# Scan layer: one more state run filled by GpSimd, state rows of 388 columns, and the output projection in a lent PSUM bank

## The chip, the cores and the metric

The kernel runs as one program on one core of a Trainium2 chip. The time is device time in microseconds (us), the median over several executions. Engines are named as in the profile: PE is TensorE (PEld its weight loads), DVE is VectorE, ACT is ScalarE, POOL is GpSimd, and SP is SyncE, which here does nothing but issue DMAs.

## The reference

The network has four layers on an input of 3 images with 256 channels of 48 x 48. Only the last, a selective scan (Mamba) layer, is touched:

```python
xz = einsum('blc,dc->bld', xn, in_proj_w); x_in, z = split(xz, 2)   # 512 channels each
u = silu(conv1d(x_in) + conv_b)                                     # 4 taps, causal
dt_raw, B_ssm, C_ssm = split(einsum('bld,ed->ble', u, x_proj_w))    # 16, 16, 16
dt = softplus(einsum('blr,dr->bld', dt_raw, dt_proj_w) + dt_proj_b)
A = -exp(A_log)                                                     # 512 x 16
def step(h, inp):                                                   # h: batch x 512 x 16
    h = h * exp(dt_t[:, :, None] * A) + dt_t[:, :, None] * B_t[:, None, :] * u_t[:, :, None]
    return h, einsum('bdn,bn->bd', h, C_t)
y = (ys + u * D_param) * silu(z)
out = einsum('bld,cd->blc', y, out_proj_w)                          # 256 channels, plus the residual x
```

The sequence of an image has 2304 tokens. Everything is fp32.

## The kernel before

The sequence is cut into chunks of 384 tokens (CH), 6 an image, 18 in all. A chunk has four channel blocks m of 128 channels, and every block two halves h of eight states each, so a chunk has **eight steps** (m, h), called the first to the eighth step here. The code counts half steps j = 0 to 15: step (m, h) holds j = 4m + 2h and the next.

In a step the 128 partitions hold 32 channels times 4 states, and the free dimension holds 8 runs of 384 tokens, indexed (g, q): two groups g of states and four quarters q of the channel block. The tile `hs` (states, L1725, three buffers) holds the runs as rows of 385 columns: the state that is carried in and 384 tokens. One step of work on a state tile is:

- **fill** (L1745): dt\*u times B is written into all eight runs before they are scanned. DVE makes the quarters q = 0, 1 (`fill_upper`, L1736). It reads dt\*u from the PSUM tile `ps_r`, two banks, one for each quarter, which `spread_pe` (L1704) writes with two matmuls of 32 rows. For h = 0 it fills both groups of its own step and the first group of the next (1536 and 768 columns), for h = 1 the second group (768). GpSimd makes q = 2, 3 of both groups in one instruction (1536 columns, L1753). It reads dt\*u from the SBUF tile `dtur`, which `spread` (L1692) loads from the DRAM tile `dtud`.
- **decay** (L1770): ACT computes exp(dt A) of one run into one of three PSUM slots, three runs ahead of the scan.
- **scan** (L1783): DVE scans one run in place (L1786). The order is q = 0, 1 of both groups, then q = 2, 3 of both.
- **times_c** (L1790): GpSimd multiplies all 3072 columns with C into `hc` (L1803).
- **add_states** (L1808): PE sums `hc` over the states into `ps_y` (L1820), after a first matmul with the diagonal of D (L1815). **gate** (L1825) multiplies with silu(z) on DVE.
- `first_states` and `last_states` carry eight columns from chunk to chunk (ACT copies, through small tiles `hst`).

The fill of the next step is issued at the end of a step, after its eight scans, and stands before `times_c` on GpSimd.

Beside the steps, the next chunks are prepared and the last one is finished. Three lists, `after`, `plan` and `gating` (L1380 to L1430), say when: each entry has a half step j, a place in it (BEGIN, MID, DONE, LATE and PE_: after the first, second, third and fourth scan, and the end of a step or of its fourth scan), a distance in chunks, and a function. `run` (L1438) calls what is due. These functions share two PSUM banks, `bank[0]` and `bank[1]`. The ones that the prediction speaks of are: project_u (PE, L1291, at j = 8, waits for ACT's silu of u), take_dbc (ACT, L1299, which also stores B and C to DRAM and loads them spread out), project_dt (PE, 17 rows, L1317, j = 8 and 10), keep_dt (ACT copies L1338, then the stores of `dtd` and `dtud`, j = 10 and 12), less_mean (PE, L1221, j = 12), centre (ACT, L1234, L1236, j = 13), square_mean (PE, L1228, j = 13), inverse_root (ACT, L1240, L1241, j = 14) and silu of z and u (ACT, with two table loads each, j = 3 and 7).

The output projection of chunk c runs while chunk c + 1 is scanned. `project_y` (L1358) adds the residual by a matmul with the identity (L1360) and four matmuls (L1362) into `bank[mo]`, one call for each half mo of the 256 output channels; `store` (L1371) copies the bank with ACT (L1372) and issues the DMA to the output:

```python
        (5, BEGIN, -1, lambda k: project_y(k, 0)),
        (6, MID, -1, lambda k: store(k, 0)),
        (7, PE_, -1, lambda k: project_y(k, 1)),
        (8, MID, -1, lambda k: store(k, 1)),
```

`keep_order` (L1889) fixes the order of PE, DVE, ACT and GpSimd to that in which the code issues its instructions; waits between engines are derived from the tiles that instructions read and write.

## Time and profile before

| what | us |
|---|---|
| median of 3 runs | 3424.14 (3421.64 to 3425.53) |
| the profiled execution | 3426.41 |
| span of the profile | 3424.6 |
| first scan begins, last scan ends | 2022.1, 3404.3 |
| busy over the span | PE 3055.3, DVE 2927.2, ACT 2378.6, POOL 1353.6 |

The profile's page gives the busy tenths of each engine in 40 slices of 85.6 us; the scan layer is the last 16 or so. Rows of groups give source line, engine, operation, names (out<-in), shapes and count, then the busy time in us, the mean of one in ns, and the idle time of the engine ahead of them with what ended it. Rows of waits give who waited for whom: us in total, how often, the longest. Rows of a timeline give start, length from the first start to the last end, engine, line, names, shape, count, and in brackets the idle time ahead. A matmul in fp32 shows as two records.

### The profile page before, as it was taken

The numbers are of one execution on the slowest core, as the hardware profiler recorded it, in microseconds if no ns is written. First come the engines' busy times: TensorE is split into PE (matmuls) and PEld (weight loads), VectorE is DVE, ScalarE is ACT, GpSimd is POOL, SyncE is SP. The second block draws the span as 40 slices with busy tenths as digits, with TensorE's granted clock in tenths as the row PEclk, the third lists the DMA queues.
The fourth block names the chain that finished last, engine by engine and source line by source line (L and its number), as shares of the span: only waits on it lengthen the run. The fifth ranks groups of instructions, "written<-read, shape, count | busy, mean of one in ns | idle before, by whom it ended". The sixth has DMA issues, their size and how long they took to land.

```text
span 3424.6 us, 51520 instructions
## 1 busy us (share of the span) xinstructions
PE 3055.3 (89%) x19882; PEld 1444.2 (42%) x19882; DVE 2927.2 (85%) x3302; ACT 2378.6 (69%) x3596; POOL 1353.6 (40%) x385
## 2 busy tenths in 40 slices
PE   7999999999999999879999978777888888877885
PEld 4334343453333435447677743333333333333331
DVE  3799899959999896479965369999999999999998
ACT  2688888848888885332224458888778888888874
POOL 0000000000000000210000039999999999999997
PEclk9999999999999999989999998888888988988887
DMA  4000000010000002756501134444454444445441
GB/s 165 28 8 10 8 8 6 12 42 5 9 9 8 7 8 82 245 165 222 192 22 37 45 104 105 110 108 122 114 121 107 116 103 113 111 109 123 121 116 43
DMA packets 167170, 272.89 MB, mean 80 GB/s; under 512 B 30129, under 2 KB 134641, under 8 KB 164994
## 3 DMA queue, kind: packets, MB, share of 16 engines
q1 hardware_dynamic: 153682, 249.44, 27.1%
q10 hardware_dynamic: 13232, 20.06, 1.8%
q8 instruction: 158, 2.59, 0.3%
q14 instruction: 98, 0.80, 0.1%
HBM read 222.08 MB, written 47.10 MB: 79 GB/s over the span
## 4 chain that ended last, share of the span: by engine, by line
PE 57%; DVE 28%; ACT 8%; issue 3%; DMA 2%; POOL 0%; SPq 0%; ACTq 0%; DVEq 0%; POOLq 0%
DVE hs L1786 17%; PE ps_s L638 16%; PE acc L651 14%; PE ps_c L1532 8%; DVE hs L1739 3%; PE ps_g L1272 3%; PE ps_g L1221 3%; PE ps_s L1031 2%; ACT ps_da L1778 2%; DVE u L296 2%; PE ps_y L462 2%; PE ps_m L665 1%; PE ps_m L711 1%; PE acc L529 1%; PE ps_s L518 1%
## 5 line engine op out<-in xcount | busy, mean ns | idle before, releaser
L642 ACT ACTIVATE pt<-ps_s 128x1024 f32<-128x1024 f32 x972 | 942.4, 1022 | 154.8 <-PE ps_s L638 142.0
L1786 DVE TENSOR_TENSOR_SCAN hs<-ps_da,hs 128x385 f32<-128x385 f32 x1152 | 1005.3, 937 | 35.2 <-ACT ps_da L1778 34.2
L857 DVE TENSOR_TENSOR part<-part,pt 128x2048 f32<-128x2048 f32 x396 | 906.6, 2289 | 41.3 <-ACT pt L642 18.5
L1778 ACT ACTIVATE ps_da<-dtr,u 128x384 f32<-128x384 f32 x1152 | 657.5, 582 | 222.9 <-DVE hs L1786 212.0
L164 POOL TENSOR_TENSOR rstd<-ve,mhalf 128x2 f32<-128x2 f32 (+1 forms) x26 | 16.3, 629 | 1479.2 <-DVE ve L162 1479.2
L638 PE MATMUL ps_s<-q,kt 32*128 32x512 f32 (+1 forms) x4320 | 576.4, 592 | 0.1
L651 PE MATMUL acc<-pt,vt 128*32 128x512 f32 (+1 forms) x4320 | 520.9, 561 | 0.2
L1803 POOL TENSOR_TENSOR hc<-hs,x 128x3072 f32<-128x3072 f32 x72 | 444.0, 6167 | 47.0 <-DVE hs L1786 38.4
L1803 POOL TENSOR_TENSOR hc<-hs,bc 128x3072 f32<-128x3072 f32 x71 | 438.0, 6169 | 42.3 <-DVE hs L1786 35.8
L1532 PE MATMUL ps_c<-vt,u 128*128 128x288 f32 x1728 | 430.4, 410 | 20.8 <-DVE u L263 20.8
L1532 PEld LDWEIGHTS ps_c<-vt,u 128*128 128x128 f32 x1728 | 329.5, 192 | 116.8 <-issue 19.7
L638 PEld LDWEIGHTS ps_s<-q,kt 32*128 32x128 f32 x4320 | 195.3, 183 | 199.1 <-issue 120.2
L1820 PE MATMUL ps_y<-hc,u 128*32 128x384 f32 x2304 | 255.4, 568 | 12.4 <-POOL hc L1803 12.4
L651 PEld LDWEIGHTS acc<-pt,vt 128*32 128x32 f32 x4320 | 94.4, 108 | 353.4 <-issue 326.7
L1272 PE MATMUL ps_g<-u 128*128 128x384 f32 x576 | 199.4, 494 | 21.3 <-ACT u L1268 21.2
L1753 POOL TENSOR_TENSOR hs<-dtur,x 128x1536 f32<-128x1536 f32 x72 | 209.1, 2905 | 7.5 <-DMA dtur<-dtud 7.5
L1753 POOL TENSOR_TENSOR hs<-dtur,bc 128x1536 f32<-128x1536 f32 x72 | 209.4, 2908 | 0.0
L1317 PE MATMUL ps_g<-wconv,u 17*128 17x384 f32 x144 | 79.2, 684 | 104.7 <-ACT x L1338 79.1
L1272 PEld LDWEIGHTS ps_g<-u 128*128 128x128 f32 x576 | 106.9, 190 | 110.8 <-ACT u L1268 42.6
L1221 PE MATMUL ps_g<-wconv,u 128*128 128x384 f32 x144 | 86.1, 770 | 63.4 <-ACT x L1338 62.9
L1820 PEld LDWEIGHTS ps_y<-hc,u 128*32 128x32 f32 x2304 | 65.5, 119 | 174.7 <-issue 153.4
L1739 DVE TENSOR_TENSOR hs<-ps_r,x 128x768 f32<-128x768 f32 (+1 forms) x108 | 127.7, 1209 | 2.9 <-DMA xd<-vt 2.8
(249 smaller groups left out, 3699.8 us busy)
## 6 DMA issues: line engine op xcount, KB each, us to landing
wconv<-in_we SPq DMA_DIRECT2D x144, 384.0 KB, 4.3
dtr<-dtd SPq DMA_DIRECT2D x288, 192.0 KB, 3.8
dtur<-dtud SPq DMA_DIRECT2D x288, 96.0 KB, 4.2
wconv<-xd SPq DMA_DIRECT2D x36, 384.0 KB, 4.8
x<-bcd SPq DMA_DIRECT2D x72, 192.0 KB, 5.3
dtd<-x SPq DMA_DIRECT2D x36, 384.0 KB, 4.8
bc<-bcd SPq DMA_DIRECT2D x72, 192.0 KB, 4.9
yc<-ycat ACTq DMA_DIRECT2D x18, 576.0 KB, 5.1
```

The lines of the kernel that those rows point to most:

```text
L638: nc.tensor.matmul(s[:, j, cols], kt[r, mt * P : (mt + 1) * P], q[r, :n], start=True, stop=True,)
L642: nc.scalar.activation(p[:, h0 : h0 + 2, :], s, AF.Exp)
L651: nc.tensor.matmul(acc[h * HD : (h + 1) * HD, :n], vt[:, mt, g * P + h * HD : g * P + (h + 1) * HD], p[:, h, cols], start=mt == 0, stop=mt ...
L857: ): nc.vector.tensor_tensor(part, first, p, ALU.add)
L1272: nc.tensor.matmul(bank[m % 2], w3v["taps"][:, m, tap, :], w3v["xi"][:, m % 3, tap : tap + CH], start=tap == 0, stop=tap == DCONV - 1,)
L1532: nc.tensor.matmul(pc[:, :HN], u[:, i, dy, ct, m * P : (m + 1) * P], vt[:, i, ct, dy * TW : dy * TW + HN], start=ct == 0 and dy == 0, stop ...
L1739: nc.vector.tensor_tensor(states(s)[:, lo:hi, 0:2, 1:], k.ps[:, :, :CH].unsqueeze(1).broadcast_to([P, hi - lo, 2, CH]), b_rows(s, lo, hi), ...
L1753: nc.gpsimd.tensor_tensor(states(s)[:, :, 2:4, 1:], chunks[at].rows[m][1].unsqueeze(1).broadcast_to([P, 2, 2, CH]), b_rows(s, 0, 2), ALU.mult,
L1778: nc.scalar.activation(slots[n % 3][:, 1 : CH + 1], chunks[at].rows[m][0][:, q, :], AF.Exp, scale=amat[:, col : col + 1],)
L1786: nc.vector.tensor_tensor_scan(b, slots[(8 * s + part) % 3][:, : CH + 1], b, 0.0, ALU.mult, ALU.add)
L1803: nc.gpsimd.tensor_tensor(hc, tiles[s][:, :, :, 1:], cb.broadcast_to([P, 2, 4, CH]), ALU.mult)
L1820: nc.tensor.matmul(k.y_ps[32 * q : 32 * q + 32, :CH], fold, hc[:, g, q, :], start=False, stop=h == 1 and g == 1,)
```

## The change

State tiles get rows of 388 columns, and the run begins at the second column. The tile from which GpSimd reads dt\*u starts every row at column 2. One of the eight runs of each second step (h = 1: g = 1, q = 1) is filled by GpSimd and no longer by DVE, whose fill shrinks from 768 to 384 columns; GpSimd reads it from a new tile `dtuq` with one buffer, which four more DMAs for each m load, and `dtud` keeps 96 instead of 64 partitions of dt\*u. The carried states move into the tile `gmat`, which was used by the earlier layers.

The output projection writes into the second bank of `ps_r` (`lent`), which DVE's fill of the second step of a block no longer reads. Its first half runs in the next chunk's fifth step in two parts (identity with m = 0, 1; then m = 2, 3), stored at the start of the sixth; its second half runs and is stored in the seventh step. The spread for m = 3 is therefore issued later, after the third scan of the sixth step.

```diff
-        d = k.dtud[m0] = dram.tile([P // 2, 2, CH], F32, name=f"dtud{m0}")
-        nc.sync.dma_start(d, k.dtu[P // 2 :, m0 : m0 + 2, :])
+        d = k.dtud[m0] = dram.tile([3 * P // 4, 2, CH], F32, name=f"dtud{m0}")
+        nc.sync.dma_start(d, k.dtu[P // 4 :, m0 : m0 + 2, :])
...
-    def project_y(k, mo, lo=0, hi=DI):
+    def project_y(k, mo, lo=0, hi=DI, into=None):
         if lo == 0:
-            nc.tensor.matmul(bank[mo], ident, k.ot[:, mo, :], start=True, stop=False)
+            k.y_out = bank[mo] if into is None else into
+            nc.tensor.matmul(k.y_out, ident, k.ot[:, mo, :], start=True, stop=False)
...
-        (5, BEGIN, -1, lambda k: project_y(k, 0)),
-        (6, MID, -1, lambda k: store(k, 0)),
-        (7, PE_, -1, lambda k: project_y(k, 1)),
-        (8, MID, -1, lambda k: store(k, 1)),
+        (8, MID, -1, lambda k: project_y(k, 0, 0, 2, lent[0])),
+        (9, BEGIN, -1, lambda k: project_y(k, 0, 2, DI)),
+        (10, BEGIN, -1, lambda k: store(k, 0, k.y_out)),
+        (12, BEGIN, -1, lambda k: project_y(k, 1, 0, DI, lent[0])),
+        (12, LATE, -1, lambda k: store(k, 1, k.y_out)),
...
-            at = 2 + m % 2
-            dtur = scn.tile([P, 2, 4 + CH], F32, name="dtur")[:, :, at : at + CH]
+            dtur = scn.tile([P, 2, 4 + CH], F32, name="dtur")[:, :, 2 : 2 + CH]
...
+        def spread_second(k, m):
+            t = scn.tile([P, 4 + CH], F32, name="dtuq", bufs=1)[:, 2 : 2 + CH]
+            for i in range(4):
+                r = slice(32 * i, 32 * i + 32)
+                nc.sync.dma_start(t[r], k.dtud[m & 2][:32, m & 1, :])
+            k.second[m] = t
...
             k.ps = t
+            lent[0] = t[:, 1, :CH]
...
-                tiles[s] = scn.tile([P, 2, 4, CH + 1], F32, name="hs", bufs=3)
+                t = scn.tile([P, 2, 4, CH + 4], F32, name="hs", bufs=3)
+                tiles[s] = t[:, :, :, 1 : CH + 2]
...
-                fill_upper(s, 1, 2)
+                fill_upper(s, 1, 2, 1)
+                nc.gpsimd.tensor_tensor(
+                    states(s)[:, 1, 1, 1:], chunks[at].second[m],
+                    chunks[at].bc[0][:, 3, :], ALU.mult,
+                )
...
-                t = state[m, h] = wp.tile([P, 8], F32, name=f"hst{m}{h}")
+                n = 8 * (2 * m + h)
+                t = state[m, h] = gmat[:, n : n + 8]
...
+                if part == 4 and h == 1 and s + 1 < len(steps):
+                    spread_second(chunks[steps[s + 1][0]], steps[s + 1][1])
...
+                if part == 2 and (m, h) == (2, 1):
+                    spread_pe(chunks[at], 3)
...
-            if h == 0 and s + 2 < len(steps):
+            if h == 0 and m != 2 and s + 2 < len(steps):
                 spread_pe(chunks[steps[s + 2][0]], steps[s + 2][1])
```

More of the change, by code (lines that the diff above doesn't have):

```diff
@@ L1200, in net, with __init__ @@
     class Chunk:
-        pass
+        def __init__(self):
+            self.second = {}
     whole = [psg.tile([P, 512], F32, name=f"ps_g{j}") for j in range(2)]
@@ L1356, in take_z @@
         nc.scalar.copy(k.sz[:, m, :], bank[j])
-    def project_y(k, mo, lo=0, hi=DI):
+    def project_y(k, mo, lo=0, hi=DI, into=None):
         if lo == 0:
-            nc.tensor.matmul(bank[mo], ident, k.ot[:, mo, :], start=True, stop=False)
+            k.y_out = bank[mo] if into is None else into
+            nc.tensor.matmul(k.y_out, ident, k.ot[:, mo, :], start=True, stop=False)
         for m in range(lo, hi):
             nc.tensor.matmul(
-                bank[mo], w("out", m * 256 + mo * P, P), k.sz[:, m, :],
+                k.y_out, w("out", m * 256 + mo * P, P), k.sz[:, m, :],
                 start=False, stop=m == DI - 1,
@@ L1369, in residual, with store @@
         nc.sync.dma_start(k.ot, xd[k.b][:, :, k.c * CH : (k.c + 1) * CH])
-    def store(k, mo):
-        nc.scalar.copy(k.ot[:, mo, :], bank[mo])
+    def store(k, mo, src):
+        nc.scalar.copy(k.ot[:, mo, :], src)
         nc.sync.dma_start(
@@ L1420, in net @@
         (2, MID, -1, residual),
-        (5, BEGIN, -1, lambda k: project_y(k, 0)),
-        (6, MID, -1, lambda k: store(k, 0)),
-        (7, PE_, -1, lambda k: project_y(k, 1)),
-        (8, MID, -1, lambda k: store(k, 1)),
+        (8, MID, -1, lambda k: project_y(k, 0, 0, 2, lent[0])),
[3 more added lines that the diff above has]
+        (12, LATE, -1, lambda k: store(k, 1, k.y_out)),
     ]
+    lent = [None]
     last_of_all = [(3, LATE, 0, lambda k: silu(k.sz))]
@@ L1694, in spread @@
             dtr = scn.tile([P, 4, CH], F32, name="dtr")
-            at = 2 + m % 2
-            dtur = scn.tile([P, 2, 4 + CH], F32, name="dtur")[:, :, at : at + CH]
-            for t, src in ((dtr, k.dtd), (dtur, k.dtud)):
-                src = src[m & 2][:, m & 1, :]
+            dtur = scn.tile([P, 2, 4 + CH], F32, name="dtur")[:, :, 2 : 2 + CH]
+            for t, src, q in ((dtr, k.dtd, 0), (dtur, k.dtud, 1)):
+                src = src[m & 2][32 * q :, m & 1, :]
                 for i in range(4):
@@ L1727, in states, with b_rows, fill_upper @@
             if s not in tiles:
-                tiles[s] = scn.tile([P, 2, 4, CH + 1], F32, name="hs", bufs=3)
+                t = scn.tile([P, 2, 4, CH + 4], F32, name="hs", bufs=3)
+                tiles[s] = t[:, :, :, 1 : CH + 2]
             return tiles[s]
-        def b_rows(s, lo, hi):
+        def b_rows(s, lo, hi, nq=2):
             at, m, h = steps[s]
             rows = chunks[at].bc[0][:, 2 * h + lo : 2 * h + hi, :]
-            return rows.unsqueeze(2).broadcast_to([P, hi - lo, 2, CH])
-        def fill_upper(s, lo, hi):
+            return rows.unsqueeze(2).broadcast_to([P, hi - lo, nq, CH])
+        def fill_upper(s, lo, hi, nq=2):
             k = chunks[steps[s][0]]
             nc.vector.tensor_tensor(
-                states(s)[:, lo:hi, 0:2, 1:],
-                k.ps[:, :, :CH].unsqueeze(1).broadcast_to([P, hi - lo, 2, CH]),
-                b_rows(s, lo, hi), ALU.mult,
+                states(s)[:, lo:hi, 0:nq, 1:],
+                k.ps[:, 0:nq, :CH].unsqueeze(1).broadcast_to([P, hi - lo, nq, CH]),
+                b_rows(s, lo, hi, nq), ALU.mult,
             )
@@ L1832, in net @@
         k.rows = {0: spread(k, 0)}
+        spread_second(k, 0)
         spread_pe(k, 0)
@@ L1882, in net @@
         for mo in range(2):
+            k.y_out = bank[mo]
             project_y(k, mo, DI - 1, DI)
-            store(k, mo)
+            store(k, mo, bank[mo])
         keep_order(tc, listed, mark)
```

## The prediction

> **What bounds the kernel now.** I read the page's slices first, then the busy times of the scan stage (first scan at 2022 us, last one ending at 3404 us), then who waits for whom in it.

> ```profile
> DVE  3799899959999896479965369999999999999998
> POOL 0000000000000000210000039999999999999997
> PEclk9999999999999999989999998888888988988887
> ...
> 2022.00:3405.00 1383.00, 1098.85 (x4583) 479.04 (x4583) 1345.46 (x1591) 1099.03 (x2134) 1292.02 (x289) 0.87 0.46 109
> ```

> The last row gives length, then busy PE, PEld, DVE, ACT, POOL, granted clock, DMA share and GB/s. DVE works 1345 of 1383 us and bounds the stage; GpSimd follows with 1292. PE is far from full, and its clock is below 1 only here.

> ```profile
> DVE hs L1786 <- ACT ps_da L1778: 34.2, 46, 0.9
> ...
> POOL hc L1803 <- DVE hs L1786: 74.2, 66, 2.9
> ```

> All that DVE waits for is ACT, some 2 us a chunk: 0.73 before the fourth scan of the third step; in the eighth step 0 to 0.9 before the fourth scan and 0.7 to 0.8 before the sixth. Consecutive chunks begin at 2720.56, 2798.15 and 2876.00, so a chunk takes about 77.7 us (every third 76.6). I work one chunk out, that of 2798.15; its eight steps begin at 2798.15, 2805.81, 2815.61, 2824.21, 2834.01, 2841.69, 2853.61 and 2863.41.

> **The run that GpSimd takes over.**

> ```profile
> L1739 DVE TENSOR_TENSOR hs<-ps_r,x 128x768 f32<-128x768 f32 x72 | 67.7, 940 | 2.8 <-DMA xd<-vt 2.8
> L1739 DVE TENSOR_TENSOR hs<-ps_r,bc 128x1536 f32<-128x1536 f32 x36 | 62.9, 1748 | 0.0
> ...
> L1803 POOL TENSOR_TENSOR hc<-hs,bc 128x3072 f32<-128x3072 f32 x71 | 438.0, 6169 | 42.3 <-DVE hs L1786 35.8 <-POOL hs L1753 6.5
> L1753 POOL TENSOR_TENSOR hs<-dtur,bc 128x1536 f32<-128x1536 f32 x72 | 209.4, 2908 | 0.0
> ```

> 768 more columns cost DVE 808 ns, so 384 fewer save 0.40 us; four times a chunk 1.6, in 18 chunks 29 us. That is the most that the change can bring. GpSimd makes a fill at 2908/1536 = 1.89 ns a column, so the new run costs 0.73 us, 2.9 a chunk: 1292 + 52 = 1344 us, still under DVE's total. The run is needed at the fourth scan of its step, while GpSimd in the fifth step ends its fill at 2841.6, five scans before the first use. I cost it at nothing; without that cover it would cost up to its own 2.9 a chunk.

> [...]

> **Rows of 388.** The product with C reads state rows of 385 columns at 2.01 ns a column; the fill reads rows of 388 at 1.89. If the stride makes the difference, the product falls to 5.81 us, 2.9 a chunk on GpSimd. No row shows these operands in the new layout, so the bounds are 5.81 and, the same difference upward, 6.53. I take the fill's rate, the nearest row with that stride. On the path it is worth 0 at 5.81 and at 6.17; at 6.53 GpSimd would need 72.1 + 2.9 + 2.9 = 77.9 a chunk and become the bound.

> **New transfers.** Four issues more for each m (0.43 us each on SP by L1701's 1.73 for four), 16 a chunk, 7 us on a queue that is mostly idle. Having one buffer, each group waits until GpSimd has read the old run, which is over more than a step earlier; store, residual and bcd issues behind it are not held. Landing takes 4.2 us (dtur's row), the use is over a step away: 0. The write of dtud grows by half, beside other work: 0. So do the state copies into gmat, same ACT copies: 0.

> **The moved output projection** is where the time goes. In the built program the TensorE order of the fifth step is: project_u; identity and m = 0, 1 of the output projection; project_dt, which waits for ACT's take_dbc; then m = 2, 3; then the sums of C. And DVE's fill at that step's end, which had no wait, now waits for the last of these matmuls: it reads bank 0 and they write bank 1 of one and the same tile. Behind that fill stand the eight scans of the sixth step, and for them ACT's decays.

> ```profile
> 2826.95 0.91 PE L1709 MATMUL ps_r<-x,u 32*128 32x384 f32 x4
> 2827.79 0.91 PE L1360 MATMUL ps_g<-wconv,ident 128*128 128x384 f32 x2
> 2828.54 2.74 PE L1362 MATMUL ps_g<-sz,u 128*128 128x384 f32 x8
> 2831.62 0.91 PE L1815 MATMUL ps_y<-x,diag 128*128 128x384 f32 x2 [0.33 <-DVE x L1827]
> 2832.46 1.50 PE L1820 MATMUL ps_y<-hc,u 128*32 128x384 f32 x16
> 2834.58 2.82 PE L1291 MATMUL ps_g<-u 128*96 128x384 f32 x8 [0.62 <-ACT u L1285]
> 2838.97 1.55 PE L1317 MATMUL ps_g<-wconv,u 17*128 17x384 f32 x4 [1.57 <-ACT wconv L1299]
> 2840.46 2.00 PE L1820 MATMUL ps_y<-hc,u 128*32 128x384 f32 x16
> ...
> 2848.40 2.92 PE L1317 MATMUL ps_g<-wconv,u 17*128 17x384 f32 x4 [4.37 <-ACT x L1338]
> 2851.25 1.65 PE L1815 MATMUL ps_y<-x,diag 128*128 128x384 f32 x2
> 2852.83 2.53 PE L1820 MATMUL ps_y<-hc,u 128*32 128x384 f32 x16
> 2859.47 5.49 PE L1221 MATMUL ps_g<-wconv,u 128*128 128x384 f32 x8 [4.11 <-ACT x L1338]
> ```

> Each fp32 matmul is two records, 0.323 us apart (L1362). *Lower end*: project_u ends at 2837.3; six records make 2839.2; project_dt 1.55, 2840.8; four records and 0.16 drain, 2842.2. DVE comes to the fill at 2840.84: **a wait of 1.35**.

> *Upper end*: the fourth step loses L1360 and L1362. TensorE, which paused 0.33 there, has nothing from the end of L1709 (2827.9 at the latest; about 2825.2, as L1709 then waits only for DVE's fill ending at 2824.2) to 2831.62: 3.8 to 6.4 us. After gaps of 4.37 and 4.11 the rows run at half speed: L1317 2.92 for 1.55, L1815 1.65 for 0.91, L1820 2.53 for 1.50, L1221 5.49 for L1291's 2.82. L1815 and L1820 would then end 1.3 later, project_u would start at 2835.9, and the wait is **2.65** (5.2 if project_u is slow as well). I take **2.2**, nearer to the slow end because the likelier gap, 6.4, is longer than both that were followed by slow rows.

> ```profile
> 2834.00:2841.70 7.70, 5.55 (x28) 2.30 (x28) 7.70 (x11) 7.30 (x15) 7.70 (x3) 0.98 0.27 70
> 2841.70:2853.60 11.90, 7.54 (x26) 2.49 (x22) 11.83 (x16) 9.72 (x20) 11.63 (x3) 0.50 0.53 114
> ```

> The granted clock falls to 0.50 right after 2841.7, with no earlier gap over 1.57 us. [...]

> The second half of the projection opens the seventh step, into L1221's gap. L1221 then runs warm and ends 2.7 earlier, which removes the fourth scan's wait in the eighth step (0, 0.6, 0.9 by chunk: 0.5). But L1228 after it may now start cold (1.56 more); I charge one in five, 0.3. The two ACT copies only change place: 0.

> **The sum, per chunk.** Fills -1.6. Of these, the first step's 0.40 returns as a longer wait in the third, since TensorE runs from 2798 to 2815 without a gap over 0.6 and feeds the ACT chain that ends there: +0.4. The seventh's returns likewise, as the ACT chain of the eighth step starts at the seventh's last scan: +0.4. New wait +2.2; eighth step -0.5 + 0.3. Total +1.2; 17 chunks make 20, and the first chunk, with no output projection behind it, gives 1 back: +19. Profiled: 3426.4 (span 3424.6 and 1.8 around it) + 19 = 3445; for the median of 3424.1, **3443 us**.

> **Rivals.**
> 1. *Faster.* TensorE stays warm in the fourth step and the two 0.4s do not return: -1.6 + 1.35 - 0.5 = -0.75 a chunk, 3410; without any wait 3395. For it: DVE is the bound and loses 29 us of work. Against: the wait is in the program. With both 0.4s returned it decides from a wait under 0.6 a chunk on, with both kept from one under 1.4. Chance 0.14.
> 2. *Nothing.* Wait at its lower end, the rest as forecast: -1.6 + 0.8 + 1.35 - 0.2 = +0.35 a chunk, 3429. Chance 0.13.
> 3. *GpSimd becomes the bound.* The product at 6.53 or the new run well over 0.73: 77.9 plus gaps a chunk; with the new wait, 3465 to 3480. Chance 0.06. If instead 388 columns do nothing (6.17), the time stays 3443, as GpSimd has room.

> **How the numbers follow.** The forecast, 3430 to 3460 (wait 1.6 to 3.2), has 0.67. Range 3416 to 3460: it leaves out the better half of rival 1, rival 3 and the wait of 5.2. Counting 0.2% (7 us), about what can be told from no change: faster 0.14, same 0.13, slower 0.73.

> **What would show it.** Right: DVE waits for PE before the 384-column fill in 17 chunks, 1.4 to 2.7 each; L1815 and L1820 slow at the fourth step's end; the third step's ACT wait up from 0.73 to about 1.1; L1221 near 2.8 us; the product with C near 5.8. Wrong: no such wait, or DVE waiting for GpSimd.

## The result and the profile after

The changed kernel takes **3440.55 us** (median of 6 runs, 3436.85 to 3442.70) against 3424.22 of the kernel before, measured beside it: ratio 1.0051, 95% interval 1.0041 to 1.0061. It is slower by 16.3 us. The forecast was 3443.

The profiled execution took 3439.55 us, 13.1 more than that of before. The scan stage itself, from the first scan to the end of the last, grew by 16.3, from 1382.2 to 1398.5. The layers ahead, which nothing touches, differ from run to run (the first scan began between 2013.9 and 2022.6 us in the profiles of this study), so the runs below are compared by their stages too. First the slices of the page, then the stage's own row (length, then busy PE, PEld, DVE, ACT, POOL, granted clock, DMA share, GB/s):

```profile
DVE  4799899859899995589965379999999999999998
...
POOL 0000000000000000110000049889999999988897
PEclk9999999999999999999999988889999988988987
```

```profile
2017.43:3415.91 1398.48, 1096.56 (x4582) 476.02 (x4582) 1317.71 (x1590) 1103.51 (x2134) 1270.15 (x361) 0.87 0.49 121
```

VectorE has 27 us less work (1345 before), and GpSimd's work fell too, by 21 (1291 before), although it has a run more to fill in half of the steps. The stage is longer all the same: VectorE now stands idle for 81 us of it, where it was 38. Its waits, then GpSimd's, in the stage:

```profile
DVE hs L1752 <- PE ps_r L1364: 43.2, 16, 2.8
DVE hs L1804 <- ACT ps_da L1796: 33.5, 36, 1.8
...
DVE hs L1804 <- POOL hs L1770: 1.4, 3, 0.8
```

```profile
POOL hs L1766 <- DMA dtuq<-dtud: 53.6, 11, 5.7
POOL hc L1821 <- DVE hs L1804: 42.6, 20, 3.1
```

The first row is new: VectorE's fill waits 16 times for the output projection. GpSimd waits for its new transfers too, but VectorE had to wait for GpSimd only three times, 1.4 us in all: GpSimd's room absorbs it. The wait in a steady chunk is seen in two timelines, of TensorE over the fourth and fifth step (2670.43 to 2690.37), and of VectorE at the end of the fifth:

```profile
2670.66 0.91 PE L1720 MATMUL ps_r<-x,u 32*128 32x384 f32 x4 [0.26 <-DVE hs L1752]
2677.83 1.65 PE L1833 MATMUL ps_y<-x,diag 128*128 128x384 f32 x2 [6.26 <-DVE x L1845]
2679.41 2.79 PE L1838 MATMUL ps_y<-hc,u 128*32 128x384 f32 x16
2682.13 2.83 PE L1292 MATMUL ps_g<-u 128*96 128x384 f32 x8
2684.79 0.81 PE L1362 MATMUL ps_r<-wconv,ident 128*128 128x384 f32 x2
2685.44 1.45 PE L1364 MATMUL ps_r<-sz,u 128*128 128x384 f32 x4
2686.82 1.55 PE L1318 MATMUL ps_g<-wconv,u 17*128 17x384 f32 x4
2688.30 1.56 PE L1364 MATMUL ps_r<-sz,u 128*128 128x384 f32 x4
```

```profile
2689.90 0.56 DVE L1752 TENSOR_TENSOR hs<-ps_r,x 128x384 f32<-128x384 f32 x1 [2.77 <-PE ps_r L1364]
```

TensorE is idle for 6.26 us of the fourth step, then L1833 and L1838 run at half speed (granted clock 0.50; 1.65 and 2.79 us, for 0.91 and 1.50 in the kernel before), and project_u (L1292), the projection and project_dt (L1318) follow without a gap up to 2689.86. VectorE's fill starts at 2689.90.

GpSimd's new run and its product with C, and VectorE's small fill:

```profile
L1821 POOL TENSOR_TENSOR hc<-hs,x 128x3072 f32<-128x3072 f32 x72 | 405.4, 5631 | 22.0 <-DVE hs L1804 22.0
...
L1766 POOL TENSOR_TENSOR hs<-dtuq,x 128x384 f32<-128x384 f32 x36 | 31.3, 869 | 43.6 <-DMA dtuq<-dtud 33.4 <-ACT ps_da L1796 5.4 <-ACT hs L1779 4.9
```

```profile
L1752 DVE TENSOR_TENSOR hs<-ps_r,x 128x384 f32<-128x384 f32 x36 | 19.4, 540 | 21.8 <-PE ps_r L1364 21.8
```

The product costs 5.63 us instead of 6.17, the run 0.87. VectorE's fill of 384 columns costs 0.54, 0.40 less than the 768.

### The profile page after: what moved, and what is told of

It is laid out like the page before. It is cut to its first block, busy times and chain, and to the rows that moved or that the text cites. A ratio compares the mean times of both kernels' runs of the same rounds, so it can differ in the third digit from the quotient of the medians.

```text
span 3437.8 us, 52144 instructions
## 1 busy us (share of the span) xinstructions
PE 3049.4 (89%) x19882; PEld 1439.2 (42%) x19882; DVE 2901.5 (84%) x3302; ACT 2383.2 (69%) x3596; POOL 1333.5 (39%) x457
## 4 chain that ended last, share of the span: by engine, by line
PE 62%; DVE 23%; ACT 6%; DMA 3%; issue 3%; POOL 1%; SPq 0%; ACTq 0%; DVEq 0%; POOLq 0%
PE ps_s L638 16%; DVE hs L1804 14%; PE acc L651 14%; PE ps_c L1536 8%; PE ps_g L1273 3%; PE ps_y L1838 3%; PE ps_s L1031 2%; DVE u L296 2%; DVE hs L1752 2%; PE ps_y L462 2%; PE ps_m L665 1%; PE ps_g L1292 1%; PE ps_r L1364 1%; ACT ps_da L1796 1%; PE ps_m L711 1%
## 5 line engine op out<-in xcount | busy, mean ns | idle before, releaser
L1804 DVE TENSOR_TENSOR_SCAN hs<-ps_da,hs 128x385 f32<-128x385 f32 x1152 | 1005.8, 940 | 35.0 <-ACT ps_da L1796 33.5
L164 POOL TENSOR_TENSOR rstd<-ve,mhalf 128x2 f32<-128x2 f32 (+1 forms) x26 | 16.3, 629 | 1476.1 <-DVE ve L162 1476.1
L1821 POOL TENSOR_TENSOR hc<-hs,x 128x3072 f32<-128x3072 f32 x72 | 405.4, 5631 | 22.0 <-DVE hs L1804 22.0
L1821 POOL TENSOR_TENSOR hc<-hs,bc 128x3072 f32<-128x3072 f32 x71 | 400.1, 5635 | 20.6 <-DVE hs L1804 20.6
L1838 PE MATMUL ps_y<-hc,u 128*32 128x384 f32 x2304 | 264.9, 586 | 11.4 <-POOL hc L1821 11.4
L1770 POOL TENSOR_TENSOR hs<-dtur,x 128x1536 f32<-128x1536 f32 x72 | 209.3, 2908 | 7.0 <-DMA dtur<-dtud 7.0
L1838 PEld LDWEIGHTS ps_y<-hc,u 128*32 128x32 f32 x2304 | 67.2, 122 | 186.3 <-issue 151.7
L1318 PE MATMUL ps_g<-wconv,u 17*128 17x384 f32 x144 | 79.2, 684 | 65.8 <-ACT x L1339 65.2
L1752 DVE TENSOR_TENSOR hs<-ps_r,x 128x1536 f32<-128x1536 f32 (+2 forms) x108 | 113.7, 1081 | 24.4 <-PE ps_r L1364 21.8
L1752 DVE TENSOR_TENSOR hs<-ps_r,bc 128x1536 f32<-128x1536 f32 (+2 forms) x108 | 113.7, 1081 | 21.4 <-PE ps_r L1364 21.4
```

The source lines that it names most:

```text
L1752: nc.vector.tensor_tensor(states(s)[:, lo:hi, 0:nq, 1:], k.ps[:, 0:nq, :CH].unsqueeze(1).broadcast_to([P, hi - lo, nq, CH]), b_rows(s, lo, ...
L1770: nc.gpsimd.tensor_tensor(states(s)[:, :, 2:4, 1:], chunks[at].rows[m][1].unsqueeze(1).broadcast_to([P, 2, 2, CH]), b_rows(s, 0, 2), ALU.mult,
L1804: nc.vector.tensor_tensor_scan(b, slots[(8 * s + part) % 3][:, : CH + 1], b, 0.0, ALU.mult, ALU.add)
L1821: nc.gpsimd.tensor_tensor(hc, tiles[s][:, :, :, 1:], cb.broadcast_to([P, 2, 4, CH]), ALU.mult)
L1838: nc.tensor.matmul(k.y_ps[32 * q : 32 * q + 32, :CH], fold, hc[:, g, q, :], start=False, stop=h == 1 and g == 1,)
```

## The experiments

"Chunk" is the time between the starts of two consecutive chunks. Ratios are to the kernel before on the same chip. Line numbers are those of the kernel in question, so they shift by a few lines between kernels.

**The projection back at its old places.** GpSimd's run and the rows of 388 stay.

```diff
-        (8, MID, -1, lambda k: project_y(k, 0, 0, 2, lent[0])),
-        (9, BEGIN, -1, lambda k: project_y(k, 0, 2, DI)),
...
+        (5, BEGIN, -1, lambda k: project_y(k, 0)),
+        (6, MID, -1, lambda k: store(k, 0, bank[0])),
+        (7, PE_, -1, lambda k: project_y(k, 1)),
+        (8, MID, -1, lambda k: store(k, 1, bank[1])),
```

> The changed kernel with the output projection put back to its old places and banks (and the spread for m = 3 to its old place); the run that GpSimd took over, its transfers and the rows of 388 stay. Theory (the loss is VectorE's new wait for the moved projection, 2.7 us a chunk): the wait before the 384-column fill is gone, the fills' 1.6 us a chunk are kept less the 0.4 that the third step gives back and some in the eighth, so 3406 to 3418 us, below the kernel before (3424). Rival (GpSimd's added run, or its waits for the dtuq transfers, 54 us in total, is what costs): at least 3435.

Measured 3414.21 us (3410.13 to 3417.03), ratio 0.9971 (0.9962 to 0.9981); stage 1371.3. VectorE has no wait for PE, the fifth step takes 7.28 us instead of 10.16. So the moved projection costs 26 us, and the other half of the change is worth 10. It isn't worth 29: of the fills' 1.6 us a chunk, 0.4 returns in the third step, 0.3 in the sixth and 0.35 in the eighth. VectorE waits longer for ACT in its scans than before (34.2 us), and 3.1 us in take_dt (VectorE's part of dt):

```profile
DVE hs L1803 <- ACT ps_da L1795: 45.8, 50, 1.4
```

**The second half of the matmuls after the fill.** Only m = 2, 3 of the first projection move, into the sixth step.

```diff
-        (9, BEGIN, -1, lambda k: project_y(k, 0, 2, DI)),
-        (10, BEGIN, -1, lambda k: store(k, 0, k.y_out)),
+        (10, BEGIN, -1, lambda k: project_y(k, 0, 2, DI)),
+        (10, DONE, -1, lambda k: store(k, 0, k.y_out)),
```

> The changed kernel with one move: the matmuls for m = 2, 3 of the projection's first half are issued after VectorE's fill (at the start of the sixth step instead of the fifth's second half), its store two scans later. Same matmuls, same bank. Theory: the fill now waits only for m = 0, 1, which end about when VectorE arrives; wait under 0.4 a chunk instead of 2.7, and the time falls by 30 to 43 us to 3398 to 3410. Rival (the projection in these steps costs by its TensorE time or by cold matmuls, wherever in them it stands): 3430 to 3445.

Measured 3413.34 us (3409.85 to 3417.58), ratio 0.9971 (0.9959 to 0.9984); stage 1371.2. The wait is gone, and 27 us with it, 3 less than the least expected: in every second chunk 0.5 us of it comes back before the last scan of the fifth step, and the sixth step takes 12.4 to 12.7 us instead of 11.9, with a new small wait in take_dt.

```profile
DVE hs L1804 <- ACT ps_da L1796: 39.6, 51, 1.1
DVE ps_g L1334 <- ACT x L1329: 8.2, 17, 0.6
```

**Two tiles for the two banks.** The matmuls stay where the change put them, but `ps_r` becomes two tiles of one bank, so fills of two quarters are split into two instructions.

```diff
-            t = psr.tile([P, 2, 512], F32, name="ps_r")
+            t = [psr.tile([P, 512], F32, name=f"ps_r{q}") for q in range(2)]
...
-            lent[0] = t[:, 1, :CH]
+            lent[0] = t[1][:, :CH]
```

> The changed kernel with the spread in two PSUM tiles of one bank each instead of one tile of two, so the order on TensorE stays and only the wait between different banks goes. VectorE's fills of two banks become two instructions each, eight instructions more a chunk at 0.05 to 0.1 us: 7 to 14 us. Theory: no wait for TensorE before the 384-column fill although the projection still ends 3 us after VectorE arrives; 43 us less and 7 to 14 more: 3404 to 3415. Rival (whoever comes next, ACT's store of the projection at the start of the sixth step, waits as long and stalls the decays): 3425 to 3440.

Measured 3416.76 us (3412.77 to 3425.51), ratio 0.9982 (0.9972 to 0.9992); stage 1374.5: above its range by 2, and on the theory's side. Timelines of PE and of VectorE in one chunk:

```profile
2676.01 1.55 PE L1318 MATMUL ps_g<-wconv,u 17*128 17x384 f32 x4
2677.50 1.56 PE L1364 MATMUL ps_r<-sz,u 128*128 128x384 f32 x4
```

```profile
2676.30 0.54 DVE L1753 TENSOR_TENSOR hs<-ps_r,x 128x384 f32<-128x384 f32 x1
```

The fill starts 2.76 us before the projection ends, so the wait comes from the two banks being one tile in the program. The fill is over before the projection's last matmuls begin; while it reads its bank, TensorE writes project_dt (L1318) into a bank of ps_g. The price is 0.13 us in the second and in the fourth step for the split fills.

**TensorE kept busy in the fourth step.** Eight matmuls for nothing go into ps_g's second bank, which nobody reads then.

```diff
+        (6, MID, -1, for_nothing),
+        (7, BEGIN, -1, for_nothing),
         (8, MID, -1, lambda k: project_y(k, 0, 0, 2, lent[0])),
```

> The changed kernel with eight matmuls more in the fourth step, into a bank that nobody reads, in the place where TensorE now pauses 6.3 us. Theory (1.3 of the 2.7 us wait come from the halved clock): the matmul with D and the sums of C at the end of the fourth step run at full rate again (0.9 and 1.5 us instead of 1.65 and 2.8), project_u starts at +0.6 in the fifth step instead of +1.9, the wait falls to 1.3 to 1.5 a chunk and the time to 3416 to 3424. Rival (the wait comes from the order of the matmuls alone): no change, 3438 to 3445.

Measured 3437.23 us (3434.75 to 3441.20), ratio 1.0039 (1.0026 to 1.0051); stage 1394.9. The total is just under the rival's range, the wait is the theory's:

```profile
DVE hs L1813 <- ACT ps_da L1805: 50.1, 36, 2.2
DVE hs L1761 <- PE ps_r L1364: 23.2, 17, 1.4
```

The wait halves, to 1.36 us each, and the fifth step falls to 8.81. But the wait for ACT grows from 33.5 to 50.1 us: the eighth step takes 12.93 instead of 11.56, since square_mean (L1229) now runs at half speed, 2.93 us where the changed kernel has 1.56:

```profile
2715.04 2.93 PE L1229 MATMUL ps_g<-wconv,mean 128*128 128x384 f32 x4 [2.65 <-ACT wconv L1237]
```

The gap ahead of it is hardly longer than in the changed kernel (2.45). The chunk settles at 78.5 us, as without the matmuls for nothing.

**TensorE kept busy in the eighth step as well.** That run left it open whether the half speed of square_mean had eaten the gain, or whether a chunk settles at 78.5 whatever one does. Two more matmuls for nothing go between the first copy of centre and square_mean.

```diff
+        (13, LATE, 2, for_nothing_more),
         (13, PE_, 2, square_mean),
```

> The changed kernel with the eight matmuls for nothing in the fourth step, and two more between the first copy of centre and square_mean in the eighth. Theory (the warm fourth step does save 1.35 us a chunk, and lost it only because square_mean then ran slow): square_mean at full speed, eighth step 11.56 instead of 12.93, chunk 77.1: 3411 to 3424 us. Rival (the chunk falls into step with something of 78.5 us whatever is done): 3433 to 3443 us.

Measured 3420.21 us (3417.29 to 3427.58), ratio 0.9991 (0.9982 to 1.0001); stage 1378.9. The theory holds: chunks of 77.17, fifth step 8.81, eighth 11.60, and square_mean at full speed:

```profile
2703.38 1.56 PE L1378 MATMUL ps_g<-wconv,u 128*128 128x384 f32 x4 [1.40 <-ACT wconv L1235]
2704.77 1.45 PE L1229 MATMUL ps_g<-wconv,mean 128*128 128x384 f32 x4
```

So the cold part of the wait is worth its 1.35 us a chunk (20 us of the 3440), once nothing else turns cold.

**The first projection early, the second late.** This takes the place without a wait for the one, and the place that warms less_mean (2.74 us in the changed kernel, 5.49 before) for the other.

```diff
-        (8, MID, -1, lambda k: project_y(k, 0, 0, 2, lent[0])),
-        (9, BEGIN, -1, lambda k: project_y(k, 0, 2, DI)),
-        (10, BEGIN, -1, lambda k: store(k, 0, k.y_out)),
+        (7, PE_, -1, lambda k: project_y(k, 0, 0, DI, bank[1])),
+        (8, MID, -1, lambda k: store(k, 0, k.y_out)),
```

> The changed kernel with the first output projection back at the end of the fourth step, in ps_g's second bank, and the second left in the seventh step. Theory (the fifth step's wait is the loss, and the second projection's new place is worth a quick eighth step): fifth step 7.28, sixth 12.21, eighth 11.56, so 75.9 us a chunk instead of 78.5: 3390 to 3404 us. Rival (the slow stretches of TensorE's clock only move, and the eighth step loses 1.4 us as it did with the warm fourth step): 77.3 a chunk, 3411 to 3424 us.

Measured 3410.63 us (3407.60 to 3411.28), ratio 0.9956 (0.9943 to 0.9970); stage 1368.9. It missed both ranges, the rival's by 0.4: the first seven steps are as expected, the eighth takes 11.56 in two of the 15 full chunks after the first and 12.06 to 12.93 in the others. Two consecutive chunks show why: after the same gap of 2.65 us square_mean and project_z (L1349) run at full speed in the first, and fall to half speed in the second.

```profile
2701.40 1.56 PE L1229 MATMUL ps_g<-wconv,mean 128*128 128x384 f32 x4 [2.65 <-ACT wconv L1237]
2702.79 1.45 PE L1349 MATMUL ps_g<-u 128*128 128x384 f32 x4
```

```profile
2777.30 1.81 PE L1229 MATMUL ps_g<-wconv,mean 128*128 128x384 f32 x4 [2.65 <-ACT wconv L1237]
2778.91 2.76 PE L1349 MATMUL ps_g<-u 128*128 128x384 f32 x4
```

**The same, with the eighth step kept busy**, by the line `(13, LATE, 2, for_nothing_more)` as above.

> The kernel with the first projection early (fourth step, ps_g's second bank) and the second in the seventh step, and two matmuls for nothing between the first copy of centre and square_mean in the eighth step. Theory (what that kernel lacked was a quick square_mean in two chunks of three): eighth step 11.6 in all chunks instead of 11.56 to 12.94, 75.9 us a chunk: 3393 to 3404 us. Rival (the slow stretch moves on once more, to project_z or to the steps before): 76.5 a chunk or more, 3405 to 3415 us.

Measured **3397.08 us** (3395.31 to 3405.68), ratio 0.9935 (0.9922 to 0.9949); stage 1359.8, chunks of 75.93 with an eighth step of 11.60 throughout. It is the best version of this study, 25 us under the kernel before and 43 under the changed one. What VectorE still waits for is ACT:

```profile
DVE hs L1811 <- ACT ps_da L1803: 35.7, 37, 2.0
```

**Rows of 388 alone**, in the kernel before. Beside the rows, the carried states move into `gmat`, as in the change; this holds for the two kernels after it as well.

```diff
-                tiles[s] = scn.tile([P, 2, 4, CH + 1], F32, name="hs", bufs=3)
+                t = scn.tile([P, 2, 4, CH + 4], F32, name="hs", bufs=3)
+                tiles[s] = t[:, :, :, 1 : CH + 2]
```

> The kernel before with the state rows of 388 columns and nothing else of the change. Theory (the row length matters to GpSimd's product with C alone, and GpSimd isn't on the path): the product falls from 6.17 us to 5.63 as in the changed kernel, VectorE's rows keep their lengths, and the time stays: 3416 to 3431 us. Rival (GpSimd, done earlier, releases rows and products earlier, which is worth time): below 3412. Second rival (the 5.63 comes from another part of the change): the product stays at 6.17.

Measured 3423.26 us (3421.43 to 3430.10), ratio 1.000 (0.9991 to 1.0010). The product takes 5.63 us, GpSimd's other rows keep their lengths, and the time doesn't move. The part is free and alone brings nothing.

**Which part of the layout.** Two kernels, one execution each: rows of 388 with the states from column 0, and rows of 386. In the second the states begin at column 1, not 0 as the expectation says, so the product reads from column 2, as in the rows of 388.

> The kernel before with state rows of 388 columns whose states begin at column 0 instead of 1, so that the 384 columns that the product reads begin at column 1 of the row instead of 2. Theory (the length of the row decides): the product stays at 5.63 us. Rival (the place of the first column decides): it goes back towards 6.17. Time 3416 to 3431 us by both.

> The kernel before with state rows of 386 columns, states from column 0, so that the product reads from column 1. If an even row length is enough, the product takes 5.63 us; if it needs a row divisible by four, or an even first column, 6.17. Time 3416 to 3431 us by both.

Measured 3426.25 and 3424.75 us. The product with rows of 388 alone, in the first of the two, and in the second:

```profile
L1805 POOL TENSOR_TENSOR hc<-hs,x 128x3072 f32<-128x3072 f32 x72 | 405.3, 5629 | 84.8 <-DVE hs L1788 71.5 <-issue 10.8 <-DVE x L1829 1.6
```

```profile
L1805 POOL TENSOR_TENSOR hc<-hs,x 128x3072 f32<-128x3072 f32 x72 | 483.3, 6713 | 10.7 <-DVE hs L1788 8.5 <-POOL hs L1754 1.8 <-ACT ps_da L1780 0.3
```

```profile
L1805 POOL TENSOR_TENSOR hc<-hs,x 128x3072 f32<-128x3072 f32 x72 | 444.4, 6172 | 46.9 <-DVE hs L1788 38.3 <-POOL hs L1754 7.2 <-DVE x L1829 1.1
```

The row length by itself is not the cause: with 388 columns and the data one column earlier the product is slower (6.71) than with 385 (6.17). In these kernels the place of a row's first column decides (counted from the tile's start). All eight rows at 2 past a multiple of four give 5.63, all at 1 give 6.71; with 386 the rows stand at 2 and 0 in turn, with 385 at all four places, and both give 6.17, the mean of 5.63 and 6.71. The fill, which writes the same rows, takes 2.91 to 2.93 us in all of these.

**The run on GpSimd without the rows of 388**: the first experiment's kernel with rows of 385.

```diff
-                t = scn.tile([P, 2, 4, CH + 4], F32, name="hs", bufs=3)
-                tiles[s] = t[:, :, :, 1 : CH + 2]
+                tiles[s] = scn.tile([P, 2, 4, CH + 1], F32, name="hs", bufs=3)
```

> The kernel with the run on GpSimd and the output projection at its old places, but state rows of 385 columns again. Theory (the new run has room even without the faster product): GpSimd needs 72.1 + 4 x 0.87 = 75.6 us of a chunk of 76.8, still under VectorE, so the time is that of the kernel with rows of 388: 3408 to 3422 us. Rival (GpSimd becomes the bound without the 388, since it also waits some 2 us a chunk for VectorE and transfers): 77.6 us a chunk or more, 3428 us or above, and VectorE waits for POOL.

Measured 3417.18 us (3414.63 to 3420.45), ratio 0.9981 (0.9972 to 0.9991): 3 above the kernel with 388, at the edge of what can be told. The product is back at 6.17, and GpSimd's waits for VectorE all but vanish (1.0 us). In the chunks between the first and the last it is nearly the bound, and not yet: they take 76.82 us with both kinds of rows. In the last chunk, which prepares no other, GpSimd does become the bound: that chunk takes 70.8 us against 66.4 with 388, and four of the five waits of VectorE's scans for it stand there:

```profile
L1819 POOL TENSOR_TENSOR hc<-hs,x 128x3072 f32<-128x3072 f32 x72 | 444.3, 6171 | 1.0 <-DVE hs L1802 1.0
```

```profile
DVE hs L1802 <- POOL hs L1768: 4.1, 5, 1.1
```

## Why the prediction was right, and where its terms were off

The forecast of 3443 was right in sign, mechanism and size: VectorE saves work, and the fill at the end of the fifth step hands back more in a wait for the output projection. That it came so near owes something to luck, since two terms were off in opposite directions. By steps of a steady chunk (before: the mean of its three kinds, 77.38; after: 78.50), in us:

| step | forecast | measured |
|---|---|---|
| first | -0.40 | -0.40 (7.66 to 7.26) |
| third: fill, and the return as a wait for ACT | 0 | 0 (the wait 0.73 to 1.13) |
| fifth: fill and new wait | +1.8 | +2.48 (7.68 to 10.16) |
| seventh | -0.40 | -0.40 (9.79 to 9.40) |
| eighth | +0.20 | -0.57 (12.13 to 11.56) |
| sum | +1.2 | +1.12 |

- **The new wait: mis-sized.** 2.2 was taken between 1.35 (TensorE warm) and 2.65 (cold); the steady chunk shows 2.77, above the upper end (in the table, less the fill's 0.40, and with 0.1 more because the fill no longer starts before the record of the last scan ends). Both ends were nearly right, the choice between them was wrong. Warm it is 1.36, as the kernel with the busy fourth step shows. Cold it depends on more than the gap, by which the text priced it: the gap is 6.26 us in each of the 16 chunks that have the wait, yet the wait is 2.11 in the first of them, then 2.44, 2.61 and 2.69, and about 2.78 from there on. What moves is the point at which the granted clock is back at 1.00: 36.00 us after the start of the first of these chunks (2096.63), 37.43 after that of a steady one (2644.75). The rows are the two stretches at half clock (the last figures are granted clock, DMA share and GB/s) and the first of the waits:

```profile
2125.80:2132.63 6.83, 2.93 (x14) 0.97 (x18) 6.83 (x8) 5.82 (x8) 6.83 (x3) 0.50 0.64 146
2675.35:2682.18 6.83, 4.35 (x19) 1.15 (x19) 6.83 (x9) 6.10 (x10) 6.83 (x3) 0.50 0.80 175
```

```profile
2141.11 0.56 DVE L1752 TENSOR_TENSOR hs<-ps_r,bc 128x384 f32<-128x384 f32 x1 [2.11 <-PE ps_r L1364]
```

- **The eighth step: mis-sized the other way, by about as much.** The fourth scan's wait did go (0.52 on average), as less_mean ran at full speed (2.74 us). The slow square_mean, charged at one in five for 0.3, never came in the steady chunks. Of the 0.40 of the seventh's fill that was to return, 0.1 did, measured against the kernel before's chunks without that wait (11.45). Why so little was not tried.
- **So the sum is better than its terms**: +0.7 in the fifth step and -0.8 in the eighth cancel, which is luck. That square_mean can be warm or cold after the same gap of 2.65 us was in the text only as "one in five"; the busy fourth step and the early first projection show that it can be cold in all steady chunks or in most.
- **The fills' returns: right in kind.** With the projection back, the stage gains 11 us of the 29, and the rest returns. The waits that name ACT account for 15 of the 18 us (45.8 for 34.2, and the new 3.1). The 0.3 in the sixth step was not forecast.
- **GpSimd: hidden, as said.** The new run costs 0.87, not 0.73: 384 and 1536 columns at 869 and 2908 ns make, by a line through the two, 1.77 ns a column and 0.19 us for the instruction, which the rate per column left out. The product takes 5.63, below the lower bound of 5.81.
- **The rows of 388: the reason was wrong.** The text took the row's stride for the cause; it is the first column. The upper bound of 6.53 was too low as well: a first column one earlier costs 6.71.
- **New transfers at 0: right for the time, wrong in its reason.** The text had them land more than a step ahead of their use. The run for the eighth step waits 4.4 to 5.7 us in every chunk but the last (53.6 us in 11 chunks by its row in the section on the result; in the other six the profile names ACT, 30.8 us). Its transfers should start in the sixth step, but stand in SyncE's queue behind the store of dtd, which waits 4.6 us for ACT, and eight loads of B and C. The last of the four is issued at 2706.0, when GpSimd has stood idle since 2705.2. The new run stands first in its fill, so it holds GpSimd until they land, and only GpSimd's room hides it.

```profile
2697.87 3.79 SPq L1310 DMA_DIRECT2D bc<-bcd  x8
...
2703.27 3.00 SPq L1712 DMA_DIRECT2D dtuq<-dtud  x4
```

```profile
2710.16 0.87 POOL L1766 TENSOR_TENSOR hs<-dtuq,x 128x384 f32<-128x384 f32 x1 [4.96 <-DMA dtuq<-dtud]
```

- **The rivals.** "Faster" priced the kernel without any wait at 3395, which is the 29 us of the fills alone; by its own terms, -2.1 a chunk, it would have been 3388. The first three ways of taking the wait away gave 3413 to 3417, since part of the 1.6 returned in each, in different steps. Only the first projection early with the eighth step kept busy came down to it, at 3397; there 0.4 still returns in the third step and 0.3 in the sixth, and the eighth is 0.5 shorter. "Nothing", 3429 with the wait at its lower end, was 3420 when TensorE was kept warm at both places: its eighth step had been priced too high. GpSimd as the bound did not come.
- **One reading was loose.** That TensorE's clock is below 1 only in the scan stage is more than the slices show: a 9 stands for 0.9 or more, and one 8 (the slice from 1712 us) lies ahead of the stage. Nothing in the sum rests on it.

## What to carry to other kernels

Lending one bank of a PSUM tile to another engine tied its users together here, though they touch different banks (a wait of 2.77 us, gone with two tiles): make every bank a tile of its own, or place the borrower's last write after the lender's read. Where one engine feeds several chains and slows down after gaps, as TensorE did here (1.65 us for 0.91 after 6.26 idle), price a move by the gap that it leaves as well as by the gap that it fills, and put short work into the gap ahead of the chain that ends last: two spare matmuls were worth 14 us here, with the first projection early. A sum that comes out right can hide terms that are wrong by two thirds of the whole, so check it step by step.
